# Seven quarter products in place of eight in the first MLP layer of an attention and clustering block

## The chip, the cores and the metric

The kernel runs on one core of one Trainium2 chip. The metric is the device time in microseconds of one execution; lower is better. Three runs of the kernel before gave 3557.26 us as their median, from 3555.52 to 3558.32. The profile is of one further execution, which took 3556.4 us and whose span in the trace is 3554.6 us.

## What is computed

The input is an image batch x of shape (4, 256, 64, 64) in 32-bit floats, so each of the four images is a matrix of 256 channels by 4096 pixels. Layer 0 is self-attention over the pixels with a residual. Layer 1 is a group norm, a clustering step with a residual, a second group norm, a two-layer MLP with a residual, and two batch norms with a 1x1 convolution between them. Cut to what the change touches:

```python
hdn = conv1x1(group_norm(y, gn2_w, gn2_b), mlp_w1, mlp_b1)      # 256 -> 1024 channels
hdn = conv1x1(jax.nn.gelu(hdn), mlp_w2, mlp_b2)                 # 1024 -> 256
y = y + ls2[None, :, None, None] * hdn
z = relu(batch_norm(y * dw_w[None, :, None, None], dw_g, dw_b, dw_m, dw_v))
z = relu(batch_norm(conv1x1(z, pw_w), pw_g, pw_b, pw_m, pw_v))
```

A 1x1 convolution is a matrix product over the channels. The first layer is thus, for one image, a 1024 x 256 weight matrix times a 256 x 4096 matrix.

## The kernel before

**Stages.** The program is a loop over the four images b. For each it runs `weighting` (attention: the softmax weights times the values), `cluster`, and `mlp`. Each engine executes its instructions in the order in which the program issues them, which is written out by hand under `manual_schedule`; the framework adds the semaphores between engines. Work of the next image (`nxt`) is woven into the current one: its projections are handed out by `fill`, and in `mlp` one `score` call per block computes a 128 x 4 x 512 piece of the next image's attention scores. A score is four matmuls over 32 rows each, into two PSUM tiles (`halves`) of two banks each. ACT copies each half to SBUF (L332, L337), and DVE keeps a running maximum `top` straight from PSUM (L334, L336, L339). After the eighth score, `fold` (L344) folds the maxima, `maximum` calls `across`, which transposes them on PE (`tt`, L350), and `first` calls `spread` (`mb`, L364), which hands the maximum to every row.

**The MLP.** The pixels go by in eight blocks nb of 512. `norm` (L937) writes the normalised block, two rows of 128 channels, by two DVE instructions. For each of eight slices j of 128 hidden channels, PE makes two matmuls of 512 columns (L991, tile `h`) that add up in one PSUM bank, ACT applies bias and GELU into SBUF (L999, tile `hs`), and PE makes the two matmuls of the second layer (L980, tile `mo`) for the slice before, which add up over all j in the two banks `acc`. At the end of a block DVE adds the scaled result to the residual (L1018), and ACT writes a relu of it (L1021). `last` for the block before is issued within the next one, at j = 1: four matmuls `pw` (L951), two relus on ACT (L960), two stores on SyncE's queue.

**Buffers.** PSUM has eight banks: two for `acc` (`ps_a`), two for tiles of one bank (`ps_m`), and four for two tiles of two banks (`ps_s`). Tiles of a pool take its buffers in turn; a tile whose buffer is still in use makes its first writer wait.

**How matmuls are counted.** Every matmul of 32-bit floats stands in the profile as two MATMUL records and two LDWEIGHTS records. The 512 first-layer matmuls of the program are therefore 1024 records.

Of the kernel before, what the change touches and what calls it, by code (L numbers as in the profile page):

```python
# [8 lines left out]
F32 = mybir.dt.float32  # L9
# [4 lines left out]
P = 128  # L14
# [3 lines left out]
NB = 512  # L18
# [27 lines left out]
def attention_then_cluster_block(  # L46
# [100 lines left out]
    def pvc(name, p=P, off=0):  # L147
        i = PV[name] + off
        return pv_s[:p, i : i + 1]
# [14 lines left out]
    fb_w = const.tile([ED, P], F32, name="fb_w")  # L164
    wf_t = const.tile([ED, C], F32, name="wf_t")

    def derived():

        for s, e, g, v, m, b_ in (
            (dw_d, dw_e, "dw_g", "dw_v", "dw_m", "dw_b"),  # L170
            (pw_s, pw_e, "pw_g", "pw_v", "pw_m", "pw_b"),
        ):
            rsqrt(s, par(v), BN_EPS)
            nc.vector.tensor_tensor(s, s, par(g), ALU.mult)
            nc.vector.tensor_tensor(e, s, par(m), ALU.mult)
            nc.vector.tensor_tensor(e, par(b_), e, ALU.subtract)
        nc.vector.tensor_tensor(dw_d, dw_d, par("dw_w"), ALU.mult)
        nc.vector.tensor_tensor(lsb1, par("ls2"), par("mlp_b2"), ALU.mult)
        nc.vector.tensor_tensor(lsb1, lsb1, dw_d, ALU.mult)
        nc.vector.tensor_tensor(dw_e, dw_e, lsb1, ALU.add)  # L180

        nc.vector.tensor_scalar(gbv, gbv, pvc("gamma"), None, ALU.mult)
        nc.vector.tensor_scalar(ab, pv_s[:, PV["alpha"] : PV["alpha"] + 2], 0.5, None, ALU.mult)


        nc.vector.tensor_scalar(fb_w, ones[:ED], pvc("f_b", ED), None, ALU.mult)
        tps = ps_m.tile([P, NB], F32, tag="m", name="wf_p")
        for k in range(KC):
            nc.tensor.transpose(
                tps[:ED, k * P : (k + 1) * P], mix[:, k, 0, 16 : 16 + ED], ident  # L190
            )
        nc.tensor.matmul(tps[:, C : C + ED], fb_w, ident[:ED, :ED], start=True, stop=True)
        nc.vector.tensor_copy(wf_t, tps[:ED, :C])
        nc.vector.tensor_copy(fvb[:, :ED], tps[:, C : C + ED])
# [44 lines left out]
    def attention(b, xs):  # L239
# [73 lines left out]
                    out=qs[nb][g * D : (g + 1) * D], in_=own["q"][r * D : (r + 1) * D]  # L313
                )

        def score(u):

            nb, g = divmod(u, GRP)
            q_s, k_s = qs[nb], own["k"]
            s = slots[u] = spool.tile([P, RG, NB], F32, tag="s", name=f"s_{b}_{u}")  # L320
            halves = [
                ps_s.tile([P, 2, NB], F32, tag="s", name=f"sc_{b}_{u}_{h}") for h in range(2)
            ]
            for r in range(RG):
                rows = slice(r * D, (r + 1) * D)
                nc.tensor.matmul(  # L326
                    halves[r // 2][:, r % 2, :], k_s[rows, g, :], q_s[rows, :], start=True, stop=True
                )
            if g == 0:
                tops[nb] = work.tile([P, 2, NB], F32, tag="top", bufs=1, name=f"top_{b}_{nb}")  # L330
            top = tops[nb]
            nc.scalar.copy(s[:, 0:2, :], halves[0])  # L332
            if g == 0:
                nc.vector.tensor_tensor(top, halves[1], s[:, 0:2, :], ALU.max)  # L334
            else:
                nc.vector.tensor_tensor(top, halves[1], top, ALU.max)  # L336
            nc.scalar.copy(s[:, 2:4, :], halves[1])  # L337
            if g:
                nc.vector.tensor_tensor(top, halves[0], top, ALU.max)  # L339
# [3 lines left out]
            top = tops[nb]  # L343
            nc.vector.tensor_tensor(top[:, 0], top[:, 0], top[:, 1], ALU.max)  # L344

        def across(nb):
            top = tops.pop(nb)
            tp = ps_m.tile([P, 4, P], F32, tag="m", name=f"tt_{b}_{nb}")
            for j in range(4):
                nc.tensor.transpose(tp[:, j, :], top[:, 0, j * P : (j + 1) * P], ident)  # L350
            mx = small.tile([P, 4], F32, tag="mx", name=f"mx_{b}_{nb}")
            nc.vector.tensor_reduce(mx, tp, AX.X, ALU.max)
            dg = work.tile([P, 4, P], F32, tag="w", bufs=3, name=f"dg_{b}_{nb}")
            nc.vector.tensor_tensor(
                dg,
                ident.unsqueeze(1).to_broadcast([P, 4, P]),
                mx.unsqueeze(2).to_broadcast([P, 4, P]),
                ALU.mult,
            )
            return dg  # L360
# [104 lines left out]
            score(GRP)  # L465

        def maximum():
            half["dg"] = across(0)

        def first():  # L470
            spread(0, half["dg"])
# [453 lines left out]

    def mlp(b, ys, stats2, fill, nxt):

        ga, gb = group_norm(b, "gn2", stats2, fill)
        fill(N)
        ob = out[b].rearrange("(k p) h w -> p k (h w)", p=P)  # L930
        pairs = {}

        def norm(nb):

            pairs[nb] = spool.tile([P, 2, KC, NB], F32, tag="s", name=f"xn2_{b}_{nb}")
            for k in range(KC):
                nc.vector.tensor_scalar(  # L937
                    pairs[nb][:, 0, k, :],
                    block(ys, k, nb),
                    ga[:, k : k + 1],  # L940
                    gb[:, k : k + 1],
                    ALU.mult,
                    ALU.add,
                )

        def last(nb):
            zs = pairs.pop(nb)
            ps = ps_s.tile([P, 2, NB], F32, tag="s", name=f"pw_{b}_{nb}")
            for c in range(KC):
                for k in range(KC):  # L950
                    nc.tensor.matmul(  # L951
                        ps[:, c, :],
                        wpw_s[:, k, c * P : (c + 1) * P],
                        zs[:, 1, k, :],
                        start=(k == 0),
                        stop=(k == KC - 1),
                    )
            for c in range(KC):
                o_s = zs[:, 0, c, :]
                nc.scalar.activation(  # L960
                    o_s, ps[:, c, :], AF.Relu, scale=pw_s[:, c : c + 1], bias=pw_e[:, c : c + 1]
                )
                nc.sync.dma_start(out=ob[:, c, nb * NB : (nb + 1) * NB], in_=o_s)

        norm(0)
        if nxt:
            nxt.q_block(0, nc.sync)
            nxt.q_block(1, nc.sync)
        for nb in range(NBLK):
            if nb + 1 < NBLK:  # L970
                norm(nb + 1)
            xn = pairs[nb]
            acc = [
                ps_a.tile([P, NB], F32, tag=f"a{c}", name=f"mo{c}_{b}_{nb}") for c in range(KC)
            ]
            hs = []

            def second(j):
                for c in range(KC):
                    nc.tensor.matmul(  # L980
                        acc[c],
                        w2_s[:, j, c * P : (c + 1) * P],
                        hs[j],
                        start=(j == 0),
                        stop=(j == HID // P - 1),
                    )

            for j in range(HID // P):
                ps = ps_m.tile([P, NB], F32, tag="m", name=f"h_{b}_{nb}_{j}")
                for k in range(KC):  # L990
                    nc.tensor.matmul(  # L991
                        ps,
                        w1_s[:, k, j * P : (j + 1) * P],
                        xn[:, 0, k, :],
                        start=(k == 0),
                        stop=(k == KC - 1),
                    )
                h_s = work.tile([P, NB], F32, tag="w", bufs=3, name=f"hs_{b}_{nb}_{j}")
                nc.scalar.activation(h_s, ps, AF.Gelu_apprx_tanh, bias=pvc("b1", P, j))  # L999
                hs.append(h_s)  # L1000
                if j == 1 and nb:
                    last(nb - 1)
                if j:
                    second(j - 1)
                if nxt and j == 3:
                    nxt.score(nb)
                    if nb == NBLK - 1:
                        nxt.fold(0)
                if nxt and nb == NBLK - 1 and j == 6:
                    nxt.maximum()  # L1010
            second(HID // P - 1)
            if nb == NBLK - 1:
                table(AF.Exp)
                if nxt:
                    nxt.first()
            for c in range(KC):
                yb = block(ys, c, nb)
                nc.vector.scalar_tensor_tensor(  # L1018
                    yb, acc[c], par("ls2", c), yb, ALU.mult, ALU.add
                )  # L1020
                nc.scalar.activation(  # L1021
                    xn[:, 1, c, :], yb, AF.Relu, scale=dw_d[:, c : c + 1], bias=dw_e[:, c : c + 1]
                )
        if nxt:
            nxt.exps(0)
        last(NBLK - 1)
# [100 lines left out]
```

## Time and profile before

| what | value |
| --- | --- |
| median of three runs | 3557.26 us |
| span of the profiled execution | 3554.6 us |
| TensorE (PE) busy | 3467.7 us, 98% |
| VectorE (DVE) busy | 1699.8 us, 48% |
| ScalarE (ACT) busy | 1560.3 us, 44% |
| GpSimd (POOL) busy | 1380.2 us, 39% |
| the four MLP stages, start of the first `h` to the end of the last `mo` | 254.4 us each for the first three, 245.9 us for the last, which has no scores to make |
| DVE, ACT and POOL busy in the first of these | 38.4, 83.6 and 0.0 us |

A busy share is an average over the whole span. The stages differ: in the MLP the vector engines have much room, in the attention stage less. For a matmul, the profile's mean duration includes the time in which it drains while the next one is already running; its cost in a stream is the distance from one start to the next.

### The profile page before, as it was taken

How to read it: one execution, taken by the hardware profiler on the slowest of the kernel's cores; microseconds unless marked ns; L12 is line 12 of the kernel's file. 1: busy time of each engine (PE TensorE's matmuls, PEld its weight loads, DVE VectorE, ACT ScalarE, POOL GpSimd, SP SyncE). 2: the span in 40 equal slices, each digit the busy share in tenths (PEclk: the TensorE clock that was granted, in tenths of full speed). 3: DMA queues.
4: the chain of work that ended last, by engine and by line, in shares of the span. 5: the costliest groups of instructions: out<-in, count | busy, mean ns of one | idle time of the engine just before them, and what ended most of it. 6: DMA issues, size and time to landing. Idle time of an engine off the chain costs nothing.

```text
span 3554.6 us, 28614 instructions
## 1 busy us (share of the span) xinstructions
PE 3467.7 (98%) x11016; PEld 1570.0 (44%) x11016; DVE 1699.8 (48%) x1972; ACT 1560.3 (44%) x1765; POOL 1380.2 (39%) x660
## 2 busy tenths in 40 slices
PE   8999999999999999999999999999999999997899
PEld 4344445644444444654444444464444444445444
DVE  3666664411366666441146666743115666664100
ACT  4555552433454554343354554533335554542222
POOL 1565665100265665410035665631004666672000
PEclk9999999999999999999999999999999999998999
DMA  2000001000000000000000000100000000000000
GB/s 89 7 4 3 6 1 48 7 18 18 12 6 4 3 6 20 29 13 12 18 15 4 3 6 3 47 1 13 18 18 9 4 6 3 4 0 1 12 18 18
DMA packets 25368, 46.93 MB, mean 13 GB/s; under 512 B 6704, under 2 KB 8592, under 8 KB 25232
## 3 DMA queue, kind: packets, MB, share of 16 engines
q1 hardware_dynamic: 20240, 38.29, 3.2%
q10 hardware_dynamic: 4992, 6.82, 0.8%
q8 instruction: 86, 1.41, 0.2%
q14 instruction: 50, 0.41, 0.0%
HBM read 19.93 MB, written 16.78 MB: 10 GB/s over the span
## 4 chain that ended last, share of the span: by engine, by line
PE 94%; DVE 3%; ACT 1%; issue 0%; DMA 0%; SPq 0%; ACTq 0%
PE av L389 50%; PE h L991 13%; PE mo L980 12%; PE sc L326 8%; PE pw L951 3%; PE vp L278 2%; PE fv L762 2%; PE mb L364 1%; PE den L410 1%; PE qp L297 0%; PE kp L255 0%; PE tt L350 0%; DVE vf L771 0%; PE op L883 0%; DVE x L898 0%
## 5 line engine op out<-in xcount | busy, mean ns | idle before, releaser
L389 PE MATMUL av<-s,v 128*128 128x512 f32 x4096 | 1826.5, 597 | 1.3 <-ACT s L379 1.3
L384 POOL TENSOR_TENSOR acc<-acc,s 128x1024 f32<-128x1024 f32 x448 | 1058.3, 2362 | 470.3 <-ACT s L379 450.7
L389 PEld LDWEIGHTS av<-s,v 128*128 128x128 f32 x4096 | 758.9, 190 | 1025.3 <-issue 1015.8
L379 ACT ACTIVATE s<-s 128x1024 f32<-128x1024 f32 x512 | 539.0, 1057 | 464.6 <-DVE s L376 431.4
L336 DVE TENSOR_TENSOR top<-sc,top 128x1024 f32<-128x1024 f32 x224 | 274.2, 1224 | 714.5 <-PE sc L326 714.5
L376 DVE TENSOR_TENSOR s<-s,mb 128x1024 f32<-128x1024 f32 x512 | 595.0, 1206 | 8.6 <-PE mb L364 8.3
L381 POOL TENSOR_TENSOR acc<-s 128x1024 f32<-128x1024 f32 x32 | 75.2, 2349 | 1133.9 <-ACT s L379 1133.9
L991 PE MATMUL h<-xn,w_s 128*128 128x512 f32 x1024 | 480.9, 597 | 4.6 <-DVE xn L937 4.6
L980 PE MATMUL mo<-hs,w_s 128*128 128x512 f32 x1024 | 476.0, 592 | 0.0
L332 ACT COPY s<-sc 128x1024 f32<-128x1024 f32 x256 | 258.5, 1010 | 406.4 <-PE sc L326 406.4
L999 ACT ACTIVATE hs<-h,pv_s 128x512 f32<-128x512 f32 x256 | 176.1, 688 | 478.6 <-PE h L991 478.6
L991 PEld LDWEIGHTS h<-xn,w_s 128*128 128x128 f32 x1024 | 192.8, 191 | 255.4 <-issue 249.6
L980 PEld LDWEIGHTS mo<-hs,w_s 128*128 128x128 f32 x1024 | 194.6, 190 | 244.9 <-issue 239.2
L337 ACT COPY s<-sc 128x1024 f32<-128x1024 f32 x256 | 259.3, 1013 | 91.6 <-DVE top L336 50.3
L339 DVE TENSOR_TENSOR top<-sc,top 128x1024 f32<-128x1024 f32 x224 | 274.4, 1225 | 49.7 <-ACT s L332 30.0
L326 PE MATMUL sc<-q,k 32*128 32x512 f32 x2048 | 295.1, 640 | 2.7 <-ACT s L337 2.7
L1018 DVE SCALAR_TENSOR_TENSOR x<-mo,pc_s,x 128x512 f32<-128x512 f32 x64 | 48.1, 751 | 495.9 <-PE mo L980 492.5
L326 PEld LDWEIGHTS sc<-q,k 32*128 32x128 f32 x2048 | 81.9, 182 | 194.8 <-issue 109.1
L278 PE MATMUL vp<-wv_s,x 128*128 128x256 f32 x512 | 132.4, 407 | 21.1 <-ACT cl L908 11.7
L278 PEld LDWEIGHTS vp<-wv_s,x 128*128 128x128 f32 x512 | 98.0, 200 | 49.6 <-ACT cl L908 16.6
L951 PE MATMUL pw<-xn,wpw_s 128*128 128x512 f32 x256 | 115.5, 594 | 0.8 <-ACT xn L1021 0.8
L334 DVE TENSOR_TENSOR top<-sc,s 128x1024 f32<-128x1024 f32 x32 | 39.2, 1225 | 146.4 <-ACT s L332 146.4
(166 smaller groups left out, 1652.6 us busy)
## 6 DMA issues: line engine op xcount, KB each, us to landing
x<-in_x SPq DMA_DIRECT2D x32, 512.0 KB, 4.7
out<-xn SPq DMA_DIRECT2D x64, 256.0 KB, 2.1
q<-q ACTq DMA_DIRECT2D x104, 64.0 KB, 2.0
w_s<-in_w SPq DMA_DIRECT2D x2, 1024.0 KB, 7.6
q<-q SPq DMA_DIRECT2D x24, 64.0 KB, 2.0
wv_s<-in_wv SPq DMA_DIRECT2D x1, 256.0 KB, 6.9
wpw_s<-in_wpw SPq DMA_DIRECT2D x1, 256.0 KB, 9.5
wfv_l<-in_wfv SPq DMA_DIRECT2D x1, 192.0 KB, 3.0
```

What stands on the lines that cost most here:

```text
L278: nc.tensor.matmul(vps[0][:, i % 2, :], xs[i * P // XT][:, k, o : o + P], wv_s[:, k, :], start=(k == 0), stop=(k == KC - 1),)
L326: nc.tensor.matmul(halves[r // 2][:, r % 2, :], k_s[rows, g, :], q_s[rows, :], start=True, stop=True)
L332: nc.scalar.copy(s[:, 0:2, :], halves[0])
L336: nc.vector.tensor_tensor(top, halves[1], top, ALU.max)
L337: nc.scalar.copy(s[:, 2:4, :], halves[1])
L339: nc.vector.tensor_tensor(top, halves[0], top, ALU.max)
L376: nc.vector.tensor_tensor(sh, sh, mxs[nb].unsqueeze(1).to_broadcast([P, 2, NB]), ALU.subtract)
L379: nc.scalar.activation(sh, sh, AF.Exp)
L384: nc.gpsimd.tensor_tensor(acc, acc, s[:, 2 * h : 2 * h + 2], ALU.add)
L389: nc.tensor.matmul(av[c], own["v"][:, RG * g + quarter, c * P : (c + 1) * P], slots[u][:, quarter, :], start=(g == 0 and quarter == 0), st ...
L980: nc.tensor.matmul(acc[c], w2_s[:, j, c * P : (c + 1) * P], hs[j], start=(j == 0), stop=(j == HID // P - 1),)
L991: nc.tensor.matmul(ps, w1_s[:, k, j * P : (j + 1) * P], xn[:, 0, k, :], start=(k == 0), stop=(k == KC - 1),)
```

## The change

With the weights of the first layer cut into four quarters (upper and lower half of the input channels by lower and upper 512 hidden channels) and the block into four (upper and lower channels by left and right 256 pixels), Strassen's scheme in Winograd's form computes the product of the two by seven quarter products and sums before and after, in place of eight products.

- **Weights.** `derived`, once, forms `W_CD` and `-W_D` in place on GpSimd. `mlp` forms three more sums of 128 x 512 on GpSimd for each image, held in the three `w` buffers.
- **Input sums.** `norm` makes four 128 x 256 sums after its two scalings, on DVE for the first block and on GpSimd for the others. It is issued at j = 1 of the block before, in place of its start.
- **First layer.** `first(nb, j, todo, between)` handles two slices at once, j and j + 4, so j runs over four. Seven `product` calls of 256 columns fill three PSUM tiles, `u` and `p` in `ps_m` and `q` in `ps_s`. One ACT copy and seven DVE sums (`plus`) combine them in SBUF. Four GELUs of 256 columns, in place, replace two of 512 out of PSUM.
- **Second layer.** `second` became a generator, whose four matmuls for the pair j before are handed out by `mo(n)` between the products.
- **Block end.** The residual and relu of a block (`finish`) are issued after the next block's `first(nb, 0)`; `last` after its `first(nb, 1)`.
- **Scores.** A score is issued within j = 0 of the first block, and after j = 2 of the others. Both halves are copied by ACT, and the maxima are taken from SBUF, two (first score) or four instructions of 512 columns in place of one or two of 1024; they wait in the list `maxima` and are issued one by one by `rest`.
- **End of the stage.** `fold` and `maximum` are issued after the last block's `first(7, 3)`, ahead of its last four second-layer matmuls.

The core of the diff:

```diff
+        nc.gpsimd.tensor_tensor(W_CD, W_CD, W_D, ALU.add)
+        nc.gpsimd.tensor_scalar(W_D, W_D, -1.0, None, ALU.mult)
...
+        nc.gpsimd.tensor_tensor(w_abcd, W_CD, W_A, ALU.subtract)
+        nc.gpsimd.tensor_tensor(w_bac, w_abcd, W_D, ALU.add)
+        nc.gpsimd.tensor_tensor(w_bcd, W_B, w_abcd, ALU.subtract)
...
+            scaled(0)
+            eng.tensor_tensor(f, f, e, ALU.subtract)
+            scaled(1)
+            eng.tensor_tensor(t2, h, f, ALU.subtract)
+            eng.tensor_tensor(t3, e, t2, ALU.subtract)
+            eng.tensor_tensor(t4, t2, g, ALU.subtract)
...
+            product(p, W_A, j, e)
+            nc.scalar.copy(h1, p)
+            product(u, w_abcd, j, t2)
+            plus(h2, u, h1)
+            product(q, W_CD, j, f)
+            rest(1)
+            between()
+            mo(1)
+            product(u, w_bac, j, t3)
+            plus(h3, u, h2)
+            product(p, W_B, j, g)
+            plus(h4, q, h3)
+            plus(h2, q, h2)
+            gelu(h4, h4, hi)
+            plus(h1, p, h1)
+            gelu(h1, h1, lo)
+            mo(1)
+            product(u, W_D, j, t4)
+            plus(h3, u, h3)
+            gelu(h3, h3, hi)
+            mo(1)
+            product(q, w_bcd, j, h)
+            plus(h2, q, h2)
+            gelu(h2, h2, lo)
+            rest(1)
+            mo(2)
+            return hs
...
+        for nb in range(NBLK):
+            for j in range(4):
+                scored = nxt and j == (2 if nb else 0)
+                hs = first(
...
+                if j == 0:
+                    if nb:
+                        finish(nb - 1, acc)
...
+                if j == 1 and nb:
+                    last(nb - 1)
+                if j == 1 and nb + 1 < NBLK:
+                    norm(nb + 1, nc.gpsimd)
+                if scored and nb:
+                    nxt.score(nb, maxima)
+                todo = second(nb, acc, hs, j)
+        if nxt:
+            rest(len(maxima))
+            nxt.fold(0)
+            nxt.maximum()
+        table(AF.Exp)
+        for _ in todo:
+            pass
+        if nxt:
+            nxt.first()
+        finish(NBLK - 1, acc)
```

## The prediction

> **What bounds the kernel now.** I read the busy table first, then the chain that ended last, the groups by line and shape, and the order of time in one block of the MLP. From the page:
>
> ```profile
> PE 3467.7 (98%) x11016; PEld 1570.0 (44%) x11016; DVE 1699.8 (48%) x1972; ACT 1560.3 (44%) x1765; POOL 1380.2 (39%) x660
> ...
> PE 94%; DVE 3%; ACT 1%; issue 0%; DMA 0%; SPq 0%; ACTq 0%
> ```
>
> PE is the bound, and 94% of the chain is PE work. A matmul taken away in the MLP is worth its full time, as long as PE then has no new waits. The groups concerned:
>
> ```profile
> L991 PE MATMUL h<-xn,w_s 128*128 128x512 f32 x1024 | 480.9, 597 | 4.6 <-DVE xn L937 4.6
> L980 PE MATMUL mo<-hs,w_s 128*128 128x512 f32 x1024 | 476.0, 592 | 0.0
> ...
> L999 ACT ACTIVATE hs<-h,pv_s 128x512 f32<-128x512 f32 x256 | 176.1, 688 | 478.6 <-PE h L991 478.6
> ...
> L1021 ACT ACTIVATE xn<-x,dw_e,dw_d 128x512 f32<-128x512 f32 x64 | 52.0, 813 | 79.1 <-DVE x L1018 77.6
> L1018 DVE SCALAR_TENSOR_TENSOR x<-mo,pc_s,x 128x512 f32<-128x512 f32 x64 | 48.1, 751 | 495.9 <-PE mo L980 492.5
> ...
> L716 ACT ACTIVATE sg<-sg,ab 128x256 f32<-128x256 f32 x8 | 4.8, 600 | 0.1
> ...
> L715 DVE TENSOR_TENSOR sg<-sg,prn 128x256 f32<-128x256 f32 x8 | 3.4, 425 | 0.3
> ...
> L858 ACT COPY g<-gp 128x256 f32<-128x256 f32 x4 | 1.5, 372 | 0.4
> ```
>
> PE waits 4.6 us for `h` and never for `mo`; ACT and DVE wait for PE. The last three rows are the nearest to the new small instructions. The pace of matmuls of 512 columns stands in the chain, that of 256 columns and the place of a score in the order of time (start, length in us, number of records):
>
> ```profile
> 551.50 51.50 PE av L389 x120
> ```
>
> ```profile
> 96.68 0.99 ACT L332 COPY s<-sc 128x1024 f32<-128x1024 f32 x1
> ...
> 97.57 1.02 ACT L337 COPY s<-sc 128x1024 f32<-128x1024 f32 x1
> ...
> 680.58 3.72 PE L278 MATMUL vp<-wv_s,x 128*128 128x256 f32 x16
> ...
> 731.96 1.14 PE L326 MATMUL sc<-q,k 32*128 32x512 f32 x8
> ...
> 733.13 1.01 ACT L332 COPY s<-sc 128x1024 f32<-128x1024 f32 x1 [2.04 <-PE sc L326]
> ```
>
> 512 columns: 51.50/120 = 0.429 us from record to record, so 0.858 per matmul of two records. 256 columns: (3.72 - 0.38)/15 = 0.223, with 0.38 as one record's own length; 0.445 per matmul and not 0.429.
>
> **What the Trainium skill says.** "TensorE: Matmul & The Clock Gate", Back-to-back issue gap, gives N/2.4 + 2.5 ns per pass. With two passes per record, an estimate from that page, it is 0.429 for 512 columns, as measured, and 0.216 for 256, less than the 0.223 here. The same page, LDWEIGHTS (loading the stationary operand), prices a load by its columns, whatever the matmul's length; the trace has 190 ns for each, of 223. I read the difference as the load no longer quite hidden. "VectorE: DVE Perf Modes", The TRN2 errata, gives (N+151)/0.96 ns for a 32-bit sum: 424 ns for 256 and 691 for 512 columns; L715 has 425. That page also says that small tiles pay a fixed cost each. The first page's table calls the queues of ScalarE and VectorE strict FIFO; in the trace ACT's order is that of the program, and my two largest losses rest on it.
>
> **The gain.** Before: 512 x 0.858 = 439.3 us. After: 7 products x 4 pairs x 32 blocks = 896 x 0.445 = 398.7. Gain 40.6 (51 at the page's pace).
>
> **Throughput of the others.** A pair is two slices, j and j + 4. PE takes 7 x 0.445 + 4 x 0.858 = 6.55 us for one. DVE's seven sums take 7 x 0.42 = 2.9; ACT's copy and four GELUs 0.37 + 4 x 0.60 = 2.8. GpSimd's four sums of 128x256 are about 0.7 each (an estimate from its 128x384 at 827 ns), due 20 us later. Its three weight sums (1.3 to 1.5 each by its 128x512 rows) run before the stage, while the group norm holds up PE, and the two sums in `derived` among attention work that leaves it idle 40%. The stores and q loads keep their queue, SP; a store is issued some 3 us later in its block, nobody waits. All this: nothing. No engine is full; what costs is latency at four places.
>
> **Inside a pair.** I follow each queue with delays from the trace: PE to DVE 0.05, PE to ACT 0.10, DVE to ACT and back 0.03, DVE to PE 0.15 plus 0.06 to resume. DVE's next independent instruction starts 0.08 before the last one ends, ACT's 0.10 before (96.68 to 97.57). The first stop is the second product into `u`: it needs `plus(h2)`, which needs ACT's copy of `p`. From the pair's start the copy begins at 0.70 and ends at 1.07, the sum runs from 1.10 to 1.52, `u` is free at 1.73. PE wants it after three products and one `mo`, at 3 x 0.445 + 0.858 = 2.19. The other two reuses have 0.4 us and more in hand. So a plain pair has no stall. But that ACT copy is the first link of each pair, and the slack behind it is under 0.5 us.
>
> **A: after `finish`.** The copy for j = 1 is queued behind the two relus, behind DVE's two residual sums, behind the last sum of j = 0 and a maximum. From the start of the last product of j = 0: sum starts at 0.65, maximum 0.99, residual sums 1.60 and 2.27, the second ends 3.02; second relu 3.09 to 3.91; copy to 4.18; sum to 4.63; `u` at 4.84. PE arrives at 0.445 + 0.858 + 2.19 = 3.50. Stall 1.34. Without a waiting maximum (block 1, and the last image) 0.72. 18 x 1.34 + 10 x 0.72 = 31.3 us.
>
> **B: after a score.** ACT's two copies of 1.01 stand ahead of the pair's copy: from PE's leaving the score, 0.10 to 1.11, 1.01 to 2.02, small copy 1.92 to 2.29, sum to 2.74, `u` at 2.95 for 2.19. `q` meanwhile waits for its bank, which is inside the same 0.76. 7 x 3 x 0.76 = 16.0, less some 3 that the three stages before lose at their scores already: 13.0.
>
> **C: the first pair.** There is no `mo` to put between. On DVE, scaling ends at 0.54, a sum at 1.00, scaling at 1.46, `t2` at 1.91; its product starts at 2.12 where PE was free at 1.2: 0.9 us. The score's second half waits for the copy of the first, as `q` holds the other buffer: 1.01 and its delays, 1.4. The reuses of `u` (0.65 + 0.42 + 0.21 = 1.28 for 0.89), `q` and `p` wait 0.4, 0.35 and 0.25. 3 x 3.3 + 2.3 for the last image (no score, but 0.4 for the copy) = 12.2.
>
> **D: the end.** `fold` needs two maxima still queued after the last sum; the transposes stand ahead of the last `mo`. Sum at 0.65, maxima 0.99, 1.60, 2.21, fold ends 3.6, PE at 3.8 where it was free at 1.3: 2.5 x 3 images, and 0.6 for the last image's GELU = 8.1.
>
> **Sum.** -40.6 + 31.3 + 13.0 + 12.2 + 8.1 = +24 us on the span of 3554.6, so 3578.6. The runs lie 1 to 4 us above that span; on their median of 3557.3 it gives 3581.
>
> **Bounds.** All unseen costs are at least nothing except where a wait gives the load time to hide, so the pace lies between 0.433 (the page's) and 0.475 (groups of four records: 0.95/4 each): -11 to +27 around my value. Delays half as long again add about 2 us per image; delays a third shorter with 0.5 GELUs and 0.35 sums take off 2 to 4 per image. GELU from SBUF at 0.5 or 0.65 changes nothing else. DVE slowed by GpSimd at its port: between nothing and 4 x 0.7 us per block if DVE stood still, and then little of it on the path, since the pairs have slack; I take nothing. Together the likeliest case has 3560 to 3602.
>
> **Rivals.** *The seams are hidden* (0.22). If ACT's copy came through in time at A and B, -40.6 + 12.2 + 8.1 - 3 = -23 remain: 3534. For it: 49 seams carry 47 us, and a mean of 0.48 in place of 0.97 each would already be break-even, that is, the copy reaching DVE half a microsecond sooner. Against: six of the eight links of A are rows of this trace. *Short products are dearer* (0.08): 896 x 0.475 = 425.6 leaves a gain of 13.7 and gives 3608. For it: each product of a lone 256-column pair has one load that must come behind another short record; against: sixteen in a row keep 0.223. *A draw* (0.08): half of A and B. That the change doesn't do what it says would show as other than 1792 product records; the issued code has seven per pair, so I give it nothing.
>
> **Chances.** The likeliest case has 0.62; with the dearer products, slower has 0.70. Same, within 0.2% (7 us, about what a measurement of this kernel can tell from no change), 0.08; faster 0.22. The range of 3540 to 3604 leaves out the faster half and more of the hidden-seams case and part of the dearest.
>
> **What would show it.** Right: 1792 product records at a distance of 0.22; PE idle in the MLP, ended by DVE's sums, mostly at j = 1 and at j = 3; a block of 32.17 us (716.41 to 909.42 for six) becoming about 32.9 in the first three images and shorter, near 30.3, in the last; PE waiting some 2.5 us ahead of `tt`. Wrong: a block under 32 us with scores in it, relus and copies of ACT in another order, or PE idle ended by GpSimd.

## The result, and the profile after

The changed kernel is slower. Its median is 3590.26 us (four runs, 3587.13 to 3593.47) against 3557.79 us of the kernel before beside it (four runs), a ratio of 1.0092 with a 95% interval of 1.0075 to 1.011. That is 32 us more; 24 were forecast. The profiled span grew from 3554.6 to 3585.6 us, by 31.0.

The page of the changed kernel, its busy line and its chain by engine:

```profile
PE 3455.0 (96%) x11784; PEld 1708.7 (48%) x11784; DVE 2056.5 (57%) x2929; ACT 1680.1 (47%) x2149; POOL 1482.2 (41%) x786
...
PE 88%; DVE 6%; ACT 5%; issue 1%; DMA 0%; SPq 0%; ACTq 0%
```

PE is still the bound, but 11% of the chain is now DVE and ACT, where it was 4%: PE has begun to wait for them. PE's busy time fell by only 12.7 us, although 52 us of matmuls are gone. The busy time misleads here, since the tail of a matmul counts as busy too: in the total where no other matmul follows at once, and in a group's own figure wherever another group follows. So `mo` went from 476.0 to 526.2 us for the same 1024 records. The stages show it better. The first line is the second image's MLP before, the other two are the second and the last image's MLP after, each from the first product to the end of the last `mo` (columns: length, then busy time of PE, PEld, DVE, ACT and POOL):

```profile
1560.58:1815.01 254.43, 254.43 (x637) 110.22 (x638) 38.40 (x48) 83.62 (x112) 0.00 (x0) 1.00 0.04 15
```

```profile
1568.59:1835.13 266.54, 253.72 (x828) 145.67 (x829) 127.35 (x291) 113.39 (x208) 21.04 (x28) 0.99 0.04 14
3333.89:3576.13 242.24, 237.62 (x760) 143.90 (x760) 107.22 (x258) 97.41 (x191) 21.03 (x28) 0.99 0.04 16
```

A stage with scores became 12.1 us longer (11.2 in the first image). The last image's stage, without scores, went from 245.9 to 242.2 us: it became 3.7 us shorter. DVE is busy for 127 us of 267 and ACT for 113, so neither is full.

What PE waits for stands in the waits view, for the weight loads and for the matmuls (in total, times, longest):

```profile
PEld hu L1014 <- DVE hs L1050: 122.8, 196, 1.9
```

```profile
PE hu L1014 <- DVE hs L1050: 24.2, 28, 1.1
...
PE tt L368 <- DVE top L362: 6.6, 3, 2.2
```

Of the entries of PE and its weight loads that another engine ends, the largest by far is the product into `hu`, the bank `u`, held back by a DVE sum: the next product wants the buffer before the sum has read it. A load that starts late is not yet a late matmul, so the 122.8 us overstate the loss. The 24.2 us of the matmuls are 28 waits, one for each `finish` inside the loop: four stages of seven. In order of time, block 2 of the first image, its pair j = 1:

```profile
752.08 0.59 PE L1014 MATMUL hp<-xn,w_s 128*128 128x256 f32 x2
752.36 1.40 DVE L1083 SCALAR_TENSOR_TENSOR x<-mo,pc_s,x 128x512 f32<-128x512 f32 x2
...
752.94 0.59 PE L1014 MATMUL hq<-xn,w_s 128*128 128x256 f32 x2
753.20 1.52 ACT L1086 ACTIVATE xn<-x,dw_e,dw_d 128x512 f32<-128x512 f32 x2 [0.81 <-DVE x L1083]
753.37 1.02 PE L1021 MATMUL mo<-hs,w_s 128*128 128x512 f32 x2
754.62 0.35 ACT L1053 COPY hs<-hp 128x256 f32<-128x256 f32 x1
755.48 0.70 PE L1014 MATMUL hu<-xn,w_bac 128*128 128x256 f32 x2 [1.09 <-DVE hs L1050]
```

The product of 752.08 could be copied from 752.8 on. But the two relus of `finish` stand ahead of the copy on ACT. They wait for the residual sums on DVE until 753.20 and run until 754.72, so the copy starts at 754.62; the sum follows at 755.00, and with it the product `w_bac` at 755.48. The pair takes from 752.08 to 759.89, 7.81 us, where a plain pair such as j = 0 before it takes 6.46 (745.62 to 752.08). That is the forecast wait A: 1.35 us for a forecast of 1.34.

After `last`, and after a score, in the block before:

```profile
726.97 3.60 PE L994 MATMUL pw<-xn,wpw_s 128*128 128x512 f32 x8
...
730.41 0.59 PE L1014 MATMUL hp<-xn,w_s 128*128 128x256 f32 x2
730.61 1.45 ACT L1003 ACTIVATE xn<-pw,pw_e,pw_s 128x512 f32<-128x512 f32 x2 [3.32 <-PE pw L994]
...
731.95 0.37 ACT L1053 COPY hs<-hp 128x256 f32<-128x256 f32 x1
...
732.83 0.70 PE L1014 MATMUL hu<-xn,w_bac 128*128 128x256 f32 x2
...
737.33 1.14 PE L332 MATMUL sc<-q,k 32*128 32x512 f32 x8
738.40 0.70 PE L1014 MATMUL hp<-xn,w_s 128*128 128x256 f32 x2
738.50 1.93 ACT L341 COPY s<-sc 128x1024 f32<-128x1024 f32 x2 [0.96 <-PE sc L332]
...
740.32 0.39 ACT L1053 COPY hs<-hp 128x256 f32<-128x256 f32 x1
...
741.22 0.70 PE L1014 MATMUL hu<-xn,w_bac 128*128 128x256 f32 x2
```

From the first product of a pair to `w_bac` PE needs 2.16 us of its own (745.62 to 747.78 in a plain pair). After the score it takes 2.82, and the whole pair 7.22 (738.40 to 745.62), 0.76 more than a plain one, as forecast under B. After `last` it takes 2.42, and the whole pair 6.92 (730.41 to 737.33), some 0.46 more: this wait was not in the forecast. The first relu of `last` starts at 730.61, after all four `pw`. I had let the first start when its own two were done.

The end of the stage in the first image:

```profile
944.90 0.69 DVE L362 TENSOR_TENSOR top<-top 128x512 f32<-128x512 f32 x1
...
945.64 0.66 PE L368 MATMUL tt<-ident,top 128*128 128x128 f32 x4 [2.18 <-DVE top L362]
946.14 5.29 PE L1021 MATMUL mo<-hs,w_s 128*128 128x512 f32 x8
```

PE waits 2.18 us ahead of the transposes, as forecast under D. The four matmuls behind them take 5.29 us in place of 3.60: the trace's record of TensorE's clock has it at half from 946.3 us on, for 3.4 us, in all three stages with scores, and nowhere in the MLP stages before.

### The profile page after: what moved, and what is told of

It reads as the page before. It is cut to its first block, busy times and chain, and to the rows that moved or that the text cites. A ratio compares the mean times of both kernels' runs of the same rounds, so it can differ in the third digit from the quotient of the medians.

```text
span 3585.6 us, 31827 instructions
## 1 busy us (share of the span) xinstructions
PE 3455.0 (96%) x11784; PEld 1708.7 (48%) x11784; DVE 2056.5 (57%) x2929; ACT 1680.1 (47%) x2149; POOL 1482.2 (41%) x786
## 4 chain that ended last, share of the span: by engine, by line
PE 88%; DVE 6%; ACT 5%; issue 1%; DMA 0%; SPq 0%; ACTq 0%
PE av L407 50%; PE mo L1021 10%; PE sc L332 8%; PE hu L1014 4%; PE pw L994 3%; PE hq L1014 2%; PE hp L1014 2%; PE fv L780 2%; PE vp L284 2%; DVE hs L1050 1%; ACT s L341 1%; ACT xn L1003 1%; PE mb L382 1%; ACT xn L1086 1%; PE den L428 1%
## 5 line engine op out<-in xcount | busy, mean ns | idle before, releaser
L1021 PE MATMUL mo<-hs,w_s 128*128 128x512 f32 x1024 | 526.2, 598 | 0.2 <-ACT hs L1043 0.2
L354 DVE TENSOR_TENSOR top<-sc,top 128x1024 f32<-128x1024 f32 x203 | 248.4, 1224 | 403.2 <-PE sc L332 403.2
L1043 ACT ACTIVATE hs<-hs,pv_s 128x256 f32<-128x256 f32 x512 | 259.8, 508 | 425.2 <-DVE hs L1050 413.3
L1050 DVE TENSOR_TENSOR hs<-hu,hs 128x256 f32<-128x256 f32 x384 | 163.1, 425 | 424.1 <-ACT hs L1053 285.8
L350 ACT COPY s<-sc 128x1024 f32<-128x1024 f32 x232 | 234.3, 1010 | 359.2 <-PE sc L332 359.2
L980 POOL TENSOR_TENSOR xn<-xn 128x256 f32<-128x256 f32 x28 | 24.4, 873 | 764.1 <-DVE xn L967 406.6
L357 DVE TENSOR_TENSOR top<-sc,top 128x1024 f32<-128x1024 f32 x203 | 248.6, 1225 | 47.5 <-ACT s L350 30.0
L355 ACT COPY s<-sc 128x1024 f32<-128x1024 f32 x232 | 235.0, 1013 | 81.5 <-DVE top L354 44.0
L1050 DVE TENSOR_TENSOR hs<-hq,hs 128x256 f32<-128x256 f32 x384 | 150.9, 421 | 112.9 <-PE hq L1014 108.5
L1014 PE MATMUL hp<-xn,w_s 128*128 128x256 f32 x512 | 156.8, 388 | 4.6 <-DVE xn L967 4.6
L1014 PEld LDWEIGHTS hp<-xn,w_s 128*128 128x128 f32 x512 | 96.7, 193 | 76.5 <-issue 65.2
L284 PEld LDWEIGHTS vp<-wv_s,x 128*128 128x128 f32 x512 | 95.2, 194 | 47.6 <-ACT cl L926 16.6
```

The costliest lines, as they stand in the source:

```text
L284: nc.tensor.matmul(vps[0][:, i % 2, :], xs[i * P // XT][:, k, o : o + P], wv_s[:, k, :], start=(k == 0), stop=(k == KC - 1),)
L1014: nc.tensor.matmul(out, w[:, j * P : (j + 1) * P], x, start=True, stop=True)
L1021: yield nc.tensor.matmul(acc[c], w2_s[:, jj, c * P : (c + 1) * P], hs[:, i], start=(j == 0 and i == 0), stop=(j == HID // P // 2 - 1 and i ...
L1043: nc.scalar.activation(dst, src, act, bias=bias)
L1050: nc.vector.tensor_tensor(dst, ps, term, ALU.add)
```

## The experiments

Three groups of kernels each ran on one chip and shared their runs of the kernel before: `ubank`, `relus`, `trans` and `warm` (3555.6 us), `normdve` and the three of the last heading (3556.3), `late0` and `lastlate` (3555.3). Where a gain over the change is given, the change's own median of 3590.3 is meant, which was not run again in these groups. The kernel before took 1.5 to 2.5 us less in these groups than beside the change, and two of the four runs of the change lie near 3587 and two near 3593. So gains of 7 or 8 us are hardly clear of noise by the time alone; there the traces have to show that a wait is gone. The edits are against the changed kernel.

**A second bank for the third product.** The tile of `q` has two banks, of which one was unused.

```diff
-            q = ps_s.tile([P, 2, NB], F32, tag="s", name=f"hq_{b}_{nb}_{j}")[:, 0, :HB]
+            qq = ps_s.tile([P, 2, NB], F32, tag="s", name=f"hq_{b}_{nb}_{j}")
+            q, v = qq[:, 0, :HB], qq[:, 1, :HB]
...
-            product(u, w_bac, j, t3)
-            plus(h3, u, h2)
+            product(v, w_bac, j, t3)
+            plus(h3, v, h2)
```

> The third product of each pair (w_bac, which writes u again) goes into the unused second bank of q's tile, so that PE no longer waits for the sum that reads u; every sum, copy and GELU stays where it is. My theory: the waits after finish (1.36 us with a waiting maximum, 0.70 without), after last (0.48) and part of that after a score (0.75, of which q's own wait for its bank of about 0.5 stays) are waits for that one bank, so 18 x 1.36 + 10 x 0.70 + 28 x 0.48 + 21 x 0.25 = 50 us go: 3540, below the kernel before (3557). Rival: ACT and DVE are behind by then and PE merely waits at the next reuse (u for W_D, q for w_bcd) instead: 3580 to 3590.

Measured: 3548.48 us (15 runs, 3542.95 to 3552.5), a ratio of 0.9978 [0.997, 0.9986] to the kernel before, 42 us less than the change. Nothing but PE's permission to write a bank was altered, so waiting for that bank cost more than the 32 us by which the change is slower. The rival does not hold: the waits did not come back at the next reuse in full. A part of them did, in the pair after `finish`, where PE now waits for the copy at the second product into `p`:

```profile
760.08 0.59 PE L1014 MATMUL hq<-xn,w_bac 128*128 128x256 f32 x2
760.87 0.70 PE L1014 MATMUL hp<-xn,w_s 128*128 128x256 f32 x2 [0.20 <-ACT hs L1054]
```

The pair takes 6.92 us in place of 6.46, 18 times: that is the 8 us by which the gain fell short of 50.

**The relus behind the copy.** The DVE half of `finish` stays; its two relus are issued inside the next pair, behind the copy of `p`.

```diff
+        def shown(nb):
+            for c in range(KC):
+                yb = block(ys, c, nb)
                 nc.scalar.activation(
                     pairs[nb][:, 1, c, :],
...
+                    else (lambda: shown(nb - 1)) if nb and j == 1
```

> Only the two relus of finish are issued later on ACT: inside j = 1, behind the small copy of p. My theory: the copy stands behind the relus, so the wait after finish falls from 1.36 to about 0.25 where a maximum is queued and from 0.70 to nothing: 18 x 1.1 + 10 x 0.7 = 27 us, 3563. Rival: DVE's residual sums, or the amount of work on ACT, are what PE waits for, whatever the order: within 5 us of 3590.

Measured: 3557.02 us (12 runs, 3551.79 to 3561.1), 33 us less, more than the 27 expected and level with the kernel before (1.0002 [0.9993, 1.001]). The wait is gone altogether:

```profile
752.21 0.59 PE L1014 MATMUL hp<-xn,w_s 128*128 128x256 f32 x2
...
752.89 0.37 ACT L1053 COPY hs<-hp 128x256 f32<-128x256 f32 x1 [0.38 <-PE hp L1014]
...
753.33 1.52 ACT L1090 ACTIVATE xn<-x,dw_e,dw_d 128x512 f32<-128x512 f32 x2
...
754.36 0.62 PE L1014 MATMUL hu<-xn,w_bac 128*128 128x256 f32 x2
```

The copy comes at 752.89, the relus after it, and `w_bac` at 754.36, 2.15 us after the pair's start. The same instructions on the same engines, in another order, are worth the whole of A. With 18 waits of 1.36 and 10 of 0.70 gone, 31.5 of the 33 us are accounted for.

**The relus and stores of `last` behind the copy.** The wait that I had missed, alone.

```diff
-            for c in range(KC):
+            def store():
+                for c in range(KC):
...
+            stores.append(store)
...
+                    else (lambda: stores.pop()()) if nb and j == 2
```

> The changed kernel with the two relus and stores of last issued inside the third pair, behind its small copy; nothing else. My theory: the wait of 0.48 us after last comes from the copy standing behind two relus that start only when all four pw matmuls are done; it goes in 28 blocks: 13 us, 3577. Rival: it comes from DVE, where the next block's two scalings stand ahead of the sum: unchanged, 3590.

Measured: 3578.32 us (3577.09 to 3581.7), 12 us less; 28 x 0.48 = 13 were expected. In the trace `w_bac` comes 2.15 us after the start of the pair behind `last`, in all 28 blocks, in place of 2.42. The two scalings on DVE stayed where they were, so the rival does not hold.

**The first block's score after its third pair.**

```diff
-                scored = nxt and j == (2 if nb else 0)
+                scored = nxt and j == 2
...
-                if scored and nb:
+                if scored:
                     nxt.score(nb, maxima)
```

> The changed kernel with the first block's score after its third pair, like the other blocks' scores; nothing else. My theory: inside the first pair the score's second half waits for the copy of the first, and the score takes 3.3 us in place of 1.1; after the third pair it costs some 0.75 instead. 3 x 1.5 = 5 us, and where the waits bring a half clock in the first pair (two of three stages) that goes as well, 1 to 2 us each: 3582. Rival: PE waits in the first pair for sums either way, and only the place moves: 3590.

Measured: 3582.26 us (3578.25 to 3582.58), 8 us less. The stages with scores fell from 265.6, 266.5 and 266.5 to 262.9 us each, and no half clock is left inside them in this trace. Of this fall 1.7 us each are not due to the edit: the wait ahead of `tt` is as long as before, and only the half clock behind it is absent.

```profile
945.74 0.65 PE L368 MATMUL tt<-ident,top 128*128 128x128 f32 x4 [2.19 <-DVE top L362]
946.23 3.60 PE L1021 MATMUL mo<-hs,w_s 128*128 128x512 f32 x8
```

The edit itself accounts for some 5 us: about 1 us in each stage, and 0.9 us for each of the two half clocks that fell into a first pair of the change. In the changed kernel the score within the first pair had taken two separate turns of the full length, because its second half had to wait for the copy of the first:

```profile
688.04 1.13 PE L332 MATMUL sc<-q,k 32*128 32x512 f32 x4
689.25 1.01 ACT L341 COPY s<-sc 128x1024 f32<-128x1024 f32 x1 [2.12 <-PE sc L332]
690.31 1.13 PE L332 MATMUL sc<-q,k 32*128 32x512 f32 x4 [1.14 <-ACT s L341]
691.37 0.70 PE L1014 MATMUL hu<-xn,w_bac 128*128 128x256 f32 x2
```

From 688.04 to 691.37 are 3.33 us, where an undivided score takes 1.07. Four records over two row groups cost as much as eight over four.

**Two second-layer matmuls ahead of the transposes.**

```diff
             nxt.fold(0)
+            next(todo)
+            next(todo)
             nxt.maximum()
```

> At the end of the stage two of the last four second-layer matmuls go ahead of the transposes tt. My theory: PE's wait of 2.18 us ahead of tt goes, less about 0.4 for the last GELU, in three stages: 5 us; and with the wait goes the half clock of 3.4 us that follows it and costs 1.7 us each time: 5 us more, 3580. Rival on the clock: it falls for another reason (the transposes, or the lighter use of the array in the stage): 5 us only, 3585, and the half clock stays in the trace.

Measured: 3583.21 us (3582.2 to 3584.25), 7 us less. The wait ahead of `tt` is gone (0.2 us remain ahead of the two matmuls that were moved up, and 0.44 behind the stage), and so is the half clock at the end of all three stages. That alone does not settle the rival on the clock: `late0` keeps the wait, and has no half clock there either. The last section counts all runs. The sum is short of 10, in part because other half clocks moved: one of 6.8 us now stands early in the first stage, at 696.9 us.

**Matmuls in the wait.** Two matmuls that add nothing to the output keep PE busy while it waits.

```diff
             nxt.fold(0)
+            idle = ps_m.tile([P, NB], F32, tag="m", name=f"idle_{b}")
+            for _ in range(2):
+                nc.tensor.matmul(idle, ones, w_abcd, start=True, stop=True)
             nxt.maximum()
```

> The wait ahead of tt stays; two matmuls of 512 columns whose result nobody reads are put into it (1.7 us of the 2.18). My theory of the clock: an idle PE brings the half clock, so it stays away and the last four matmuls take 3.4 in place of 5.3 us less tail: 1.7 x 3 = 5 us, 3585. Rival: the clock falls anyway, or the added matmuls push the transposes back: 3590 or a little more.

Measured: 3589.67 us (3581.85 to 3590.75), no gain outside the spread. Inside the stage the expectation held:

```profile
950.42 1.88 PE L1132 MATMUL idle<-w_abcd,ones 128*128 128x512 f32 x4
...
952.77 0.66 PE L368 MATMUL tt<-ident,top 128*128 128x128 f32 x4 [0.47 <-DVE top L362]
953.26 3.60 PE L1021 MATMUL mo<-hs,w_s 128*128 128x512 f32 x8
```

The transposes come no sooner, yet the four matmuls after them are back at 3.60 us, and the second stage lost 1.7 us (266.54 to 264.86). That fits the theory that idleness brings the half clock, and the count over all runs in the last section supports it. That the sum did not follow is put down to half clocks elsewhere, which is argued and not shown: in all they come to 95.6 us in this trace and 91.6 in that of the change, and where they fall differs from run to run.

**Input sums on DVE.** A test of another explanation, that GpSimd's new work slows DVE.

```diff
-                    norm(nb + 1, nc.gpsimd)
+                    norm(nb + 1, nc.vector)
```

> The changed kernel with the four input sums of every block on DVE in place of GpSimd. My theory: GpSimd's sums cost nothing, and DVE has room for four more of 0.42 us per block in the stretch of the four pw matmuls: 3590, within 4 us. Rival: GpSimd's traffic slows DVE's sums at the shared memory: some us faster, and shorter DVE sums in the trace.

Measured: 3592.94 us (3591.75 to 3593.98), 3 us more and not less, within the spread of the change's own runs. The DVE sums out of `hu`, `hq` and `hp` take 425, 420 and 413 ns, against 425, 421 and 413 with the sums on GpSimd. No slowing of these sums shows.

**Together.** Three kernels add the remedies up: bank and transposes; with those, a second-layer matmul ahead of the product into `q` in the pair after a score; and with that, the relus and the first score.

```diff
+            if j == 3:
+                mo(1)
             product(q, W_CD, j, f)
             rest(1)
             between()
-            mo(1)
+            if j < 3:
+                mo(1)
```

> The second bank for the third product and the later transposes together. My theory: two separate waits, so their gains add up: 42 and 7 us off 3590, 3541. Rival: both gains come from the same slack (a PE that is less behind, or the same half clock), and together they give little more than the bank alone: 3548.

> As ub_trans, and in the last pair of each block one second-layer matmul goes ahead of the third product into q. My theory: after a score, q waits for its bank until ACT has copied the first half of the score; in the run with the second bank that still costs about 0.3 to 0.4 us, 21 times, 7 to 8 us: 3534. Rival: the second-layer matmul then waits for the last GELU of the pair before, and nothing is won: 3541.

> As ub_trans_moq, and the relus of finish behind the small copy (as in relus), and the first block's score after its third pair in place of inside its first. My theory: the second bank left a wait of about 0.43 us for ACT's copy after finish where a maximum is queued (18 x 0.43 = 8 us), and the split score costs the first pair about 2.3 us (3 x 2.3 = 7 us): 3519, more than 1% below the kernel before. Rival: the first pair waits for its sums anyway, and the score only moves the time: 3526.

Measured: 3542.41, 3536.78 and 3516.92 us, ratios of 0.9962 [0.9947, 0.9977], 0.9947 [0.9932, 0.9961] and 0.9889 [0.9874, 0.9904] to the kernel before. The times lie within 3 us of those expected: the gains add up, which they would not do if two of the remedies removed the same wait. The last kernel is 39 us faster than the kernel before and 73 us faster than the change, with the same seven products. Its second image's MLP stage:

```profile
1549.82:1793.52 243.70, 242.25 (x829) 146.02 (x829) 124.67 (x291) 112.98 (x208) 21.07 (x28) 1.00 0.04 16
```

It takes 243.7 us in place of 254.4 before and 266.5 in the change, with DVE and ACT as busy as in the change (125 and 113 us): nothing was made cheaper, PE alone waits less.

## Why the prediction was right

The direction and the mechanism were right: seven products do save time on PE, and more than that is lost where ACT's small copy comes late and a bank cannot be written. The size, +24 for +32, came closer than its terms. By the steps of the prediction:

| step | forecast, us | measured, us |
| --- | --- | --- |
| the gain: 896 products for 512 matmuls | -40.6 | -52 |
| A: after `finish` | 31.3 | 31.5 (the relus run took off 33) |
| after `last` | 0 | 21 x 0.46 + 7 x 0.37 = 12 (the run took off 12) |
| B: after a score | 13.0 | 21 x 0.79 = 16.6, less 24 x 0.20 = 4.8 in the stages before: 12 |
| C: the first pair, three images | 9.9 | 14.5 |
| D: the end, three images | 7.5 | 11.6 |
| C and D of the last image | 2.9 | 1.6, by difference |
| sum | +24 | +31; the spans differ by 31.0 |

- **The gain** was mis-sized. In the changed kernel the products stand 0.43 us apart (752.08 to 752.51), two records of 0.216. My 0.223 was a mean over sixteen `vp` records. Taken one by one in the trace before, they start 0.216 apart from the third on (680.90, 681.11, 681.33); the first step alone is 0.32, just after matmuls of another shape. I had read a change-over as a pace. The price that the Trainium skill gives ("TensorE: Matmul & The Clock Gate", Back-to-back issue gap), which I had set aside, was the right one if its 2.5 ns are taken once per record of two passes: 2 x 256/2.4 + 2.5 = 216 ns, an estimate from that page. Once per pass, as the prediction words it, would give 218. The page calls this the gap of a single matmul and says that a stream can differ from it; here the stream keeps it. My reading that the load is no longer quite hidden was wrong: 7 x 4 x 32 x 0.432 = 387, so the gain is 439 - 387 = 52.
- **A and B** were right to a few hundredths of a microsecond for each wait, and so was the strict order of ACT's queue on which they rest. One link was not: PE starts 0.06 us after the sum ends (755.42 to 755.48) and not 0.21, but its two records then stand 0.32 apart in place of 0.216, so that nearly the same sum comes out. What the stages before lose at a score was taken too low: a block took 32.17 us with a score and 30.90 without (the last image), and 1.07 of the difference are the score itself; that leaves 0.20.
- **After `last`** is what the sentence that a plain pair has no stall, and the list of four places, left out. The slack of under half a microsecond was known; that both relus wait for the last `pw` was not. In the last image the wait is 0.37 us and not 0.46.
- **C** was mis-sized: each half of the split score takes as long as the whole. The first image's first pair goes from 685.64 to 693.97, 8.33 us, of which 7 x 0.432 + 1.07 = 4.1 are PE's own; that leaves 4.2 for a forecast of 3.3. Two images lose 0.9 more each, at half clocks that fall into this pair (1574.3 and 2458.4 us): 3 x 4.24 + 1.8 = 14.5.
- **D** had the wait nearly right, 2.18 for 2.5, and lacked the clock that follows it in this trace, 1.7 us each time: 3 x 3.87 = 11.6. The 1.7 us are not a fixed cost: the five other kernels that keep the wait lack them at 9 of their 15 stage ends.
- **The last image** was not taken apart. Its stage became 3.7 us shorter; with 13.1 of gain, 5.2 for A and 2.6 after `last`, 1.6 remain for its first pair and its end.
- **No engine is full**, as forecast: DVE 127 and ACT 113 us of 266.5. GpSimd's sums cost nothing, as `normdve` shows. The GELU of 256 columns took 508 ns and not my 600, which moved nothing, since it is not on the path.

The errors of gain and losses had opposite signs, which is why the sum came out better than its parts: the gain was 12 us larger than forecast and the wait that was left out cost 12. That these two cancel is luck. The 7 us by which the forecast fell short are mostly C and D. A block with a score takes 32.92 us and one of the last image 30.38, against forecasts of 32.9 and 30.3; that is so near for the same reason.

Of the rivals, the hidden seams fell with the trace. It was close to what could be had, though: with the seams really hidden the same products give 3517, below the 3534 of that rival, which still carried C and D and the slower pace. Dearer short products were wrong altogether, and a draw, with half of A and B, fell since A came in full.

## What to carry to other kernels

A saving on the busiest engine holds only while its buffers come free in time, so follow each bank that is written again back to the instruction that frees it, and count everything queued ahead of that instruction on its own engine. Where the chain is late by a microsecond, an order in which the short instruction goes first, or one spare bank, can be worth nearly as much as the work that was saved: here 33 and 42 us beside 52. And take a pace from single records, not from a group's length, which includes the change-over at its head.

## What was not expected of the hardware

- PE idle for 2.18 us at the end of a stage was followed by 3.4 us at half clock, in three stages of three in the trace of the change. Over all traces it is half of the cases. `ubank`, `relus`, `normdve`, `late0` and `lastlate` leave this wait as it is (2.18 or 2.19 us), and of the 18 stage ends in these and the change 9 have the half clock. In each trace all changes of TensorE's clock lie on a grid of 3.413 us, to within 0.003 us, and the grid lies differently from run to run. The 9 ends with the half clock are those in which 2.02 us or more of the wait lay within one step of the grid; in the other 9 the wait was cut by a step's edge, and at most 1.99 us lay within one. Where the wait is filled (`warm`) or gone (`trans` and the three kernels that hold its edit), none of 15 ends has the half clock. The waits of 1.1 us after `finish` brought none in the trace of the change. It is no rule for every place: the half clock at 1574.3 us, in a first pair, follows a step with only 1.14 us of idle, which also holds the divided score. Why it came there is open.
- The Trainium skill ("TensorE: Matmul & The Clock Gate", Part 1: The HAM clock gate) lets the clock fall only after at least one idle window of about 3.4 us. The traces agree on the length of the step, but 2.02 us of idle within one step were enough; here the measurement decides.
- A score divided into two times two row groups took 1.06 us for its second half (690.31 to 691.37), as much as all four together (737.33 to 738.40). The first half has a record of the same length.
